# Selective scan: the column directions read runs of 8 neighbours, and copies, last spread and fifth piece stand elsewhere in the step

## The chip, the cores and the metric

The kernel runs on 1 core of a Trainium2 chip. The metric is the device time of one execution in microseconds. The core's engines are named as in the profile: PE (TensorE; PEld is its weight load), DVE (VectorE), ACT (ScalarE), POOL (GpSimd) and SP, which issues the DMAs. All data is float32.

## The reference

Eight images of 64 x 64 pixels with 96 channels go through four residual layers. Layers 0 and 2 are selective scans in four directions, layer 1 is a chunked scan, and layer 3 is a spectral layer. The change lies in layers 0 and 2:

```python
# u: [192, 64*64] after in_proj, 3x3 depthwise convolution and silu
x_wh = swapaxes(u)                       # directions 1 and 3 go down the columns
xs = stack(u, x_wh, flip(u), flip(x_wh))
dts, B, C = split(xs_k @ x_proj_k)       # 6, 16 and 16 rows for each direction k
delta = softplus(dts @ dt_w_k + bias)
h = exp(delta * A) * h + (delta * x) * B # one state for each of 192 channels x 16
y_k = sum_n h * C + D * x
y = y_0 + flip(y_2) + back(y_1) + back(flip(y_3))
x = x + out_proj(layernorm(y) * silu(z))
```

## The kernel before

**Tiles and loops.** An image's `u` and `y` stay in SBUF as `[96, 2, 4096]`: two halves of 96 channels, pixels in row order. `selective_scan` runs 32 *steps*: direction `k` from 0 to 3, and 8 chunks of 512 positions in each (`LC = 512`). For `k` 1 and 3 (the *column steps*; `wh` is true) a chunk is 8 columns of 64 pixels. `view` hands out such a chunk in the order of the scan, that is with 64 pixels of one column, 256 bytes apart, before the next column.

A step has six *units* (`n` in the loop at the end), each of 32 channels x 4 of the states on the 128 partitions and 4 groups of the states along the free axis. A unit has two scans on DVE (`scan`, L870, parts `p` 0 and 1, two groups each). The input `da` is made by ACT (`decays`, L855, two activations for each part) in PSUM, in one buffer for each part, so that the next unit's `da` can only be written when this unit's scan has read it. The other input `db` is du x B (`with_b`, L840): for units 2 and 5 POOL makes it from a copy that DMA has spread over the partitions (`du2`), for units 0, 1, 3 and 4 DVE makes it one unit ahead from `pu`, which PE spreads with two matmuls (`spread`, L834). After its scan ACT copies the last state (`leave`, L886), and POOL multiplies h by C in place (L891). `enter` (L826) puts the carried state into a later `db`.

`total_y(i, hf)` sums three units: two matmuls add the old `y` (or the skip of `u`) into `py` (L898), then 24 matmuls in eight rounds, three at a time in 32 partitions each, add h x C (L908). An ACT copy writes `py` back to `y`: L993 for the first half, L1007 for the second. The sum of units 0 to 2 is issued in unit 3, that of units 3 to 5 in unit 0 of the next step. There are 5 buffers for `h`, so unit 2 of a step takes the one that the last y sum reads.

**The next step's inputs.** `prepare(i)` is a generator that the loop calls on in parts (`prepare_part`): project `u` to the delta of the second half (four matmuls, L742) and copy it to `raw` (L747), project to the first half's delta, B and C (L751) and copy (L755), send B and C to DRAM (`bcd`, L757) and read `b` back over all partitions (four DMAs, L764), softplus (L775, with two table loads) and `dd` to DRAM, read `dx` back for three units and `c` (L782, L764), `du` on POOL (L793 in column steps, L799 in row steps) with its trip through DRAM, and the second `dx`.

**Pieces beside.** From the second image on, the spectral layer of the image before is cut into pieces (`Beside`): `begin` issues a piece's matmuls into a PSUM tile, `end` its ACT operation. A call of `selective_scan` has 139 pieces in layer 0 and 137 in layer 2, so 4 or 5 (`quota`) in each of its 32 steps.

**Order.** PSUM is full: one buffer `misc` (for `pu` and some pieces), one buffer `py` (for the y sums, the projections and the other pieces), and the two `da`. The order on each engine's queue is the order of the code below, written out by hand, and each engine works its queue in that order. In a step `i`, unit by unit, before the change:

- unit 0: spread of unit 1; last y sum of step `i - 1`; scan; L755 and `b` of step `i + 1`; scan; softplus
- unit 1: spread of unit 3; scan; L1007; a piece begins on `py`; scan; it ends; first `dx` and `c`
- unit 2: a piece begins; scan; it ends, a third begins; scan; it ends
- unit 3: spread of unit 4; first y sum; scan; scan; `du` ahead of POOL's L891
- unit 4: L993; a fourth piece begins on `misc`; L742 of step `i + 2`; scan; da of unit 5; the piece ends; scan
- unit 5: a fifth piece begins on `misc`; the last spread (unit 0 of step `i + 1`); the piece ends; scan; L747 and L751; scan; second `dx` of step `i + 1`

Of the kernel before, what the change touches and what calls it, by code (L numbers as in the profile page):

```python
# [17 lines left out]
DM = 96  # L18
# [4 lines left out]
LC = 512  # L23
# [44 lines left out]
def tile_vision_stack(  # L68
# [352 lines left out]
    def view(t, wh, at, n):  # L421
# [3 lines left out]
        return t.rearrange("p (h w) -> p w h", w=64)[:, at // 64 : (at + n) // 64, :]  # L425

    def cut(t, wh):

        return t.rearrange("p (w h) -> p w h", h=64) if wh else t
# [260 lines left out]
    def selective_scan(w, wdt, a, d, u, y, beside):  # L690
# [23 lines left out]
        with (  # L714
# [14 lines left out]
            def prepare(i):  # L729

                k, c = steps[i]
                wh, at = k % 2 == 1, c * LC
                uv = [view(u[:, hf, :], wh, at, LC) for hf in range(2)]
                m = made[i] = {"dx": [], "du": []}
# [11 lines left out]
                raw = tp.tile([128, 2, LC], F32, name="raw")  # L746
                nc.scalar.copy(raw[:DM, 1, :], pv[:DM])  # L747

# [5 lines left out]
                yield  # L754
                nc.scalar.copy(raw[:, 0, :], pv)  # L755
                bcd = dp.tile([32, LC], F32, name="bcd")
# [136 lines left out]
            def total_y(i, hf):  # L893
# [6 lines left out]
                    skip[:, hf, :] if k == 0 else ident[:DM, :DM],  # L900
                    view((u if k == 0 else y)[:, hf, :], wh, c * LC, LC),
                    start=True,
# [3 lines left out]
                for g in range(NSG):  # L906
                    for q in range(3):
                        nc.tensor.matmul(  # L908
                            py[32 * q : 32 * q + 32, :],
                            red,  # L910
                            hs[q][:, g, :],
                            start=False,
                            stop=(g == NSG - 1),
                        )
                return view(y[:, hf, :], wh, c * LC, LC), cut(py, wh)

# [16 lines left out]
            with tc.tile_pool(name="p_conv", bufs=2, space=PSUM) as pvp:  # L933
# [11 lines left out]
                for hf in range(2):  # L945
                    conv(w, y, u, (0, 8), hf)
                for _ in range(5):
                    prepare_part(0)
# [4 lines left out]
                conv(w, y, u, (8, 24), 1)  # L953
                for _ in range(2):
                    prepare_part(1)
# [7 lines left out]
            with tc.tile_pool(name="p_da", bufs=1, space=PSUM) as pap:  # L963
# [12 lines left out]
                for t in range(total + 2):  # L976
# [3 lines left out]
                    if n == 2 and quota > 1:  # L980
                        other.begin(pyp, "py")
                    elif n == 5 and quota > 4:
                        other.begin(pmp, "misc")
                    if n in (0, 3, 5) and ahead:
                        spread(t + 1)
                    elif n == 1 and t + 2 < total:
                        spread(t + 2)
                    if n == 0 and i > 0:
                        sums = total_y(i - 1, 1)
                    elif n == 3:  # L990
                        sums = total_y(i, 0)
                    elif n == 4:
                        nc.scalar.copy(*sums)  # L993
                        if quota > 3:
                            other.begin(pmp, "misc")
                        prepare_part(i + 2)
                    if n == 5:
                        other.end()
                    if t < total:
# [10 lines left out]
                    elif n == 2:  # L1010
                        other.end()
                        if quota > 2:
                            other.begin(pyp, "py")
                    elif n == 4:
                        other.end()
                    elif n == 0:
                        prepare_part(i + 1)
                    elif n == 5:
                        prepare_part(i + 2)
                    if t < total:  # L1020
# [8 lines left out]
                    if n in (1, 2):  # L1029
                        other.end()  # L1030
                    if n in (0, 1, 5):
                        prepare_part(i + 1)
# [739 lines left out]
```

## Time and profile before

| | us |
|---|---|
| time, median of 3 runs | 27056.74 (27053.37 to 27074.89) |
| the profiled execution's own time | 27082.74 |
| its span in the profile | 27080.9 |
| busy: DVE, PE, POOL, ACT | 23966.2, 22624.0, 21781.7, 16539.7 |
| L870, the scans on DVE (6144) | 13765.8 busy, 900.6 idle before |
| L891, h x C on POOL (3072) | 12769.4 busy, 726.0 idle before |
| L908, the y sums on PE (24576) | 5301.4 busy, 69.9 idle before |
| L840, db on POOL (1024) and on DVE (2048) | 4648.2 and 4643.9 busy |
| mean granted clock of PE | 0.773 of full |

The profile is of one execution; busy times are the union of an engine's instructions. "Idle before" is the engine's idle time ahead of such instructions, put down to what came last. A matmul in float32 stands as two matmul instructions.

### The profile page before, as it was taken

To read this page: it belongs to the slowest core of one execution; us is meant where nothing else is said; L and a number is where in the kernel's file an instruction comes from. 1 tells how busy PE (TensorE), PEld (TensorE's weight loads), DVE (VectorE), ACT (ScalarE), POOL (GpSimd) and SP (SyncE) were. 2 spreads that over 40 slices of the span, in tenths; PEclk is the share of its full clock that TensorE was granted. 3 is DMA by queue.
4 is the path that set the end of the run, shared out by engine and by line. 5 is a ranking of instruction groups with operands and counts; after the bars stand their busy time and mean duration, and the time that the engine had idled before them with its cause. 6 is when DMAs were issued, how large, how long until landed. Compare 5 with 4: busy or idle time off the path is not lost. (4 is left out here: it accounts for less than half of the span.)

```text
span 27080.9 us, 283056 instructions
## 1 busy us (share of the span) xinstructions
PE 22624.0 (84%) x91061; PEld 8150.5 (30%) x91061; DVE 23966.2 (88%) x17105; ACT 16539.7 (61%) x29953; POOL 21781.7 (80%) x8360
## 2 busy tenths in 40 slices
PE   7787788888888888888888888888888888888888
PEld 2141122422224222242222422224222342223424
DVE  8989899798997989979898898988989889898896
ACT  5656566466665656556565565655656556565564
POOL 8949898498984979859797697976979769797694
PEclk7687777877778777787777877778777787778878
DMA  4415454154541545415453254532545325453252
GB/s 121 119 30 124 114 130 117 31 131 122 132 111 35 133 117 137 103 44 132 116 136 98 50 132 118 135 92 56 133 119 134 85 62 133 118 134 78 70 133 67
DMA packets 1681704, 2831.72 MB, mean 105 GB/s; under 512 B 434984, under 2 KB 478280, under 8 KB 1675616
## 3 DMA queue, kind: packets, MB, share of 16 engines
q1 hardware_dynamic: 1663584, 2807.32, 41.9%
q8 instruction: 730, 11.96, 0.2%
q10 hardware_dynamic: 16640, 6.29, 0.1%
q14 instruction: 750, 6.14, 0.1%
HBM read 2385.11 MB, written 427.49 MB: 104 GB/s over the span
## 5 line engine op out<-in xcount | busy, mean ns | idle before, releaser
L870 DVE TENSOR_TENSOR_SCAN h<-da,db 128x1026 f32<-128x1026 f32 x6144 | 13765.8, 2282 | 900.6 <-ACT da L855 479.2
L891 POOL TENSOR_TENSOR h<-h,c 128x2048 f32<-128x2048 f32 x3072 | 12769.4, 4174 | 726.0 <-ACT state L886 510.1
L908 PE MATMUL py<-h,cst 128*32 128x512 f32 x24576 | 5301.4, 795 | 69.9 <-POOL h L891 69.8
L855 ACT ACTIVATE da<-dx,a2s 128x512 f32<-128x512 f32 x6144 | 4236.4, 690 | 1508.7 <-DVE h L870 1366.6
L855 ACT ACTIVATE da<-dx,a0s 128x512 f32<-128x512 f32 x6144 | 4235.8, 690 | 1481.8 <-DVE h L870 1344.3
L840 POOL TENSOR_TENSOR db<-du,b 128x2048 f32<-128x2048 f32 x1024 | 4648.2, 4539 | 567.6 <-ACT db L826 567.6
L840 DVE TENSOR_TENSOR db<-pu,b 128x2048 f32<-128x2048 f32 x2048 | 4643.9, 2268 | 110.9 <-PE pu L834 100.6
L834 PE MATMUL pu<-du,cst 32*128 32x512 f32 x4096 | 3239.2, 881 | 1007.4 <-DVE db L840 799.9
L908 PEld LDWEIGHTS py<-h,cst 128*32 128x32 f32 x24576 | 1175.0, 142 | 4827.3 <-issue 4517.4
L751 PE MATMUL pv<-u,wk 96*128 96x512 f32 x2048 | 1816.9, 1030 | 688.4 <-ACT raw L747 685.8
L898 PE MATMUL py<-y,cst 96*96 96x512 f32 x1536 | 1517.0, 1084 | 397.9 <-ACT raw L755 395.4
L834 PEld LDWEIGHTS pu<-du,cst 32*128 32x128 f32 x4096 | 790.4, 239 | 3079.7 <-issue 1361.9
L742 PE MATMUL pv<-u,wk 96*96 96x512 f32 x2048 | 1452.4, 838 | 186.7 <-ACT y L993 142.6
L1285 ACT ACTIVATE sg<-sg 128x768 f32<-128x768 f32 x1024 | 819.6, 800 | 859.1 <-PE sg L1269 859.1
L993 ACT COPY y<-py 96x512 f32<-96x512 f32 x512 | 417.5, 815 | 1411.4 <-PE py L908 1411.4
L516 PE MATMUL ps<-s,w3as 96*128 96x512 f32 x1344 | 912.4, 767 | 327.7 <-ACT sf L523 188.1
L1239 POOL TENSOR_TENSOR ce<-ec,cr 112x512 f32<-112x512 f32 x256 | 530.8, 2074 | 719.1 <-ACT ec L1237 700.8
L1317 DVE TENSOR_TENSOR wt<-wt,cbm 128x768 f32<-128x768 f32 x1024 | 985.3, 997 | 136.6 <-ACT wt L1286 136.1
L886 ACT COPY state<-h 128x4 f32<-128x4 f32 x3072 | 597.5, 194 | 782.5 <-DVE h L870 776.8
L751 PEld LDWEIGHTS pv<-u,wk 96*128 96x128 f32 x2048 | 540.6, 291 | 1740.2 <-ACT raw L747 1212.5
L319 POOL TENSOR_SCALAR xn<-xs,sb 96x512 f32<-96x512 f32 x192 | 198.1, 1033 | 991.7 <-PE pz L324 495.6
L1216 POOL TENSOR_TENSOR rr<-lr,cc 128x768 f32<-128x768 f32 x256 | 376.6, 1471 | 754.1 <-ACT lr L1214 749.2
(241 smaller groups left out, 30790.9 us busy)
## 6 DMA issues: line engine op xcount, KB each, us to landing
dx<-dd SPq DMA_DIRECT2D x4096, 192.0 KB
b<-bcd SPq DMA_DIRECT2D x2048, 256.0 KB
c<-bcd SPq DMA_DIRECT2D x2048, 256.0 KB
du<-dud SPq DMA_DIRECT2D x2048, 128.0 KB
dd<-raw SPq DMA_DIRECT2D x1024, 192.0 KB
dud<-du SPq DMA_DIRECT2D x512, 128.0 KB
xd<-xs SPq DMA_DIRECT2D x256, 192.0 KB
cr<-bcd SPq DMA_DIRECT2D x1536, 32.0 KB
```

What stands on the lines that cost most here:

```text
L516: nc.tensor.matmul(ps, w3as[:, m * 128 : (m + 1) * 128], live["x2"], start=True, stop=True)
L742: nc.tensor.matmul(pv[:DM], weights[k][:, hi, 128:], uv[hi], start=(hi == 0), stop=(hi == 1))
L751: nc.tensor.matmul(pv, weights[k][:, hi, :128], uv[hi], start=(hi == 0), stop=(hi == 1))
L834: nc.tensor.matmul(pu, sel[rows, :], m["du"][rows, n // 3, :], start=True, stop=True)
L840: (nc.gpsimd if pool else nc.vector).tensor_mul(groups(m["db", n]), (m["du2"][:, n // 3, :] if pool else m["pu"]) .unsqueeze(1) .to_broadc ...
L855: nc.scalar.activation(dst[:, g, :LC], made[i]["dx"][n // 3][:, n % 3, :], AF.Exp, scale=av4[:, k, n, gs : gs + 1],)
L870: nc.vector.tensor_tensor_scan(made[i]["h", n][:, at][:, way], das[p][:, rev : 2 * SEG + rev][:, way], made[i]["db", n][:, at][:, way], 0. ...
L891: nc.gpsimd.tensor_mul(h, h, made[i]["c"])
L898: nc.tensor.matmul(py, skip[:, hf, :] if k == 0 else ident[:DM, :DM], view((u if k == 0 else y)[:, hf, :], wh, c * LC, LC), start=True, st ...
L908: nc.tensor.matmul(py[32 * q : 32 * q + 32, :], red, hs[q][:, g, :], start=False, stop=(g == NSG - 1),)
L1285: nc.scalar.activation(sg, sg, AF.Abs)
L1317: nc.vector.tensor_mul(it["wt"], it["wt"], m["cbm"][:, j : j + 1, :].to_broadcast([128, RK, Q]),)
```

## The change

In column steps, `near` reads and writes `u` and `y` row by row with runs of 8 neighbours, so `pv` and `py` hold a chunk in the order of the pixels' rows. The order of the scan is restored elsewhere: L747 and L755 read `pv` in PSUM at every eighth element (`turn_back`), and L908 writes `py` in PSUM at every eighth element, 64 elements for each of 8 columns. The copies of `py` to `y` then read PSUM in order and write runs of 8. Row steps keep their access.

In all steps, L993 stands behind the da of unit 5; L742, L747, L751 and L755 have four parts of their own, in units 4 and 5 of the step two ahead, so that L755, `bcd` and `b` come at the end of unit 5, ahead of the second `dx`; the last spread stands in unit 4, behind the beginning of the fourth piece; and the fifth piece runs on `py` from the end of unit 2 to the middle of unit 3.

```diff
+    def near(t, wh, at, n):
+        if not wh:
+            return t[:, at : at + n]
+        return t.rearrange("p (h w) -> p h w", w=64)[:, :, at // 64 : (at + n) // 64]
+
+    def turn_back(t, wh, n):
+        return t.rearrange("p (h w) -> p w h", w=n // 64) if wh else t
...
-                uv = [view(u[:, hf, :], wh, at, LC) for hf in range(2)]
+                uv = [near(u[:, hf, :], wh, at, LC) for hf in range(2)]
...
-                nc.scalar.copy(raw[:DM, 1, :], pv[:DM])
+                nc.scalar.copy(cut(raw[:DM, 1, :], wh), turn_back(pv[:DM], wh, LC))
+                yield
...
-                nc.scalar.copy(raw[:, 0, :], pv)
+                nc.scalar.copy(cut(raw[:, 0, :], wh), turn_back(pv, wh, LC))
...
-                    view((u if k == 0 else y)[:, hf, :], wh, c * LC, LC),
+                    near((u if k == 0 else y)[:, hf, :], wh, c * LC, LC),
...
-                            py[32 * q : 32 * q + 32, :],
+                            turn_back(py[32 * q : 32 * q + 32, :], wh, LC),
                             red,
-                            hs[q][:, g, :],
+                            cut(hs[q][:, g, :], wh),
...
-                return view(y[:, hf, :], wh, c * LC, LC), cut(py, wh)
+                py = py.rearrange("p (h w) -> p h w", h=64) if wh else py
+                return near(y[:, hf, :], wh, c * LC, LC), py
...
-                for _ in range(5):
+                for _ in range(6):
                     prepare_part(0)
...
-                for _ in range(2):
+                for _ in range(4):
                     prepare_part(1)
...
                     if n == 2 and quota > 1:
                         other.begin(pyp, "py")
-                    elif n == 5 and quota > 4:
-                        other.begin(pmp, "misc")
-                    if n in (0, 3, 5) and ahead:
+                    if n in (0, 3) and ahead:
                         spread(t + 1)
...
                     elif n == 4:
-                        nc.scalar.copy(*sums)
                         if quota > 3:
                             other.begin(pmp, "misc")
+                        if t + 2 < total:
+                            spread(t + 2)
                         prepare_part(i + 2)
-                    if n == 5:
-                        other.end()
+                    elif n == 5:
+                        prepare_part(i + 2)
                     if t < total:
                         scan(t, 0)
...
+                    elif n == 3:
+                        other.end()
                     elif n == 4:
+                        nc.scalar.copy(*sums)
                         other.end()
-                    elif n == 0:
-                        prepare_part(i + 1)
-                    elif n == 5:
-                        prepare_part(i + 2)
...
                     if n in (1, 2):
                         other.end()
+                        if n == 2 and quota > 4:
+                            other.begin(pyp, "py")
+                    if n in (4, 5):
+                        prepare_part(i + 2)
                     if n in (0, 1, 5):
                         prepare_part(i + 1)
```

## The prediction

> **What bounds the kernel now.** I read the page's busy rows first, then busy time in single stretches, then the waits, then the timeline of one step.
>
> ```profile
> span 27080.9 us, 283056 instructions
> PE 22624.0 (84%) x91061; PEld 8150.5 (30%) x91061; DVE 23966.2 (88%) x17105; ACT 16539.7 (61%) x29953; POOL 21781.7 (80%) x8360
> ```
>
> Two engines stand near the top, but this mixes stages. The sixteen selective scans (first to last L870 of each call) add up to 19,215 us, 37.53 us for each of 512 steps. Eight column steps and eight row steps of one call:
>
> ```profile
> core 0: us, PE busy (x) PEld busy (x) DVE busy (x) ACT busy (x) POOL busy (x), PEclk, DMA share, GB/s
> 7110.00:7410.00 300.00, 263.91 (x785) 79.82 (x785) 286.04 (x130) 208.93 (x387) 293.06 (x73) 0.75 0.54 132
> 7410.00:7710.00 300.00, 255.89 (x785) 81.09 (x784) 285.23 (x129) 204.44 (x387) 291.76 (x73) 0.74 0.53 132
> ```
>
> POOL is busy 97%, DVE 95%; over all calls POOL has 18,493 us (36.12 per step). So nothing below about 36.1 to 36.7 us per step can come from waits: nine POOL instructions a step (six L891 of 4.14 each in a chain, two L840 of 4.54, du of 2.40 or, in columns, 2.88) are 36.3 in rows and 36.8 in columns. What can be won is DVE's remaining idle:
>
> ```profile
> DVE h L870 <- ACT da L855: 479.2, 563, 7.8
> DVE h L870 <- PE py L908: 184.8, 276, 1.1
> ACT y L993 <- PE py L908: 1411.4, 477, 6.6
> ACT y L1007 <- PE py L908: 258.7, 261, 10.9
> ```
>
> Sorting the timeline's idle ahead of L870 and L840 by unit: unit 5's first scan waits 258.5 us for da, unit 2's first scan 184.8 for py (its h buffer is read by the last y sum) and 72.6 for da, unit 0's db (L840, issued in unit 5) 85.9 for pu. Unit 4 (94.5) and unit 3 (47.4) are few long waits. The timeline shows the first of these in a column step:
>
> ```profile
> 7211.30 4.48 DVE L870 TENSOR_TENSOR_SCAN h<-da,db 128x1026 f32<-128x1026 f32 x2
> 7214.99 1.07 ACT L993 COPY y<-py 96x512 f32<-96x512 f32 x1 [4.33 <-PE py L908]
> 7215.85 1.41 ACT L855 ACTIVATE da<-dx,a0s 128x512 f32<-128x512 f32 x2
> 7216.67 3.59 PE L742 MATMUL pv<-u,wk 96*96 96x512 f32 x4
> 7217.35 4.48 DVE L870 TENSOR_TENSOR_SCAN h<-da,db 128x1026 f32<-128x1026 f32 x2 [1.57 <-ACT da L855]
> ```
>
> ACT stands at the y copy while da for unit 5, whose input was free at 7213.6, queues behind it; DVE then idles 1.57 us. A row step, for the sizes:
>
> ```profile
> 339.33 0.58 ACT L993 COPY y<-py 96x512 f32<-96x512 f32 x1 [3.86 <-PE py L908]
> ...
> 339.97 1.96 PE L742 MATMUL pv<-u,wk 96*96 96x512 f32 x4 [0.75 <-ACT y L993]
> ```
>
> The same four L742 take 1.96 us in rows and 3.59 in columns, the copy 0.58 and 1.07. Over the run L742 has 592 ns (median) in rows, 1035 in columns; at half clock both read about 1060.
>
> **Part by part.**
>
> *Copies, last spread.* The y copy moves behind unit 5's first da, L755 from unit 0 to the end of unit 5, the last spread from unit 5 to unit 4. Unit 5's wait (258.5) goes: the copy no longer stands before da. The last y sum starts when POOL's sixth L891 ends and not when L755 does: at 350.77 against 352.39 + 1.96 in the row step, 3.6 us earlier, more than unit 2 waited (at most 1.1 each). So 184.8 goes, and 72.6 with it, since L1007 then finds py done. The last spread is issued some 5 us ahead of its need, so 85.9 goes. Together 601.8 us.
>
> *What these moves put in the way.* In unit 4 PE's queue now holds the fourth piece, the spread (its buffer is free when ACT has read that piece, after da and the y copy), then four L742 (free after the y copy), and ACT waits for them in L747 ahead of the next step's first da. From the column step above without its stall: da to 7215.1, copy 0.58 and piece about 0.5 to 7216.1, spread 1.12 (full clock) or 2.07 (half), L742 1.96 or 3.65, L747 0.57, da 1.42: 7221.2 or 7223.8. DVE wants it at 7211.3 + 4.4 + 4.4 + 2.4 = 7222.5. So 1.3 us early or 1.3 late. Behind the waiting L747 on ACT stand both da of the next unit 0 and the state copy that POOL's L891 waits for; the clock of 0.74 to 0.75 means half of the time at half clock. I take 0.5 us for the 7 x 64 = 448 steps with pieces: 224 us; between 0 and 1.3 x 448 = 582. The first image's 64 steps have no piece and no cost. L747 also overwrites raw, which POOL's du reads until 7214.3, five us before: no cost. The two parts more ahead of each call's loop stand beside the convolution and cost nothing.
>
> *Fifth piece.* 139 and 137 pieces on 32 steps give 11 and 9 steps with five, 140 in all. It stood ahead of the last spread and made the 85.9 us; now it stands on py ahead of unit 4's spread and the first y sum. Who waits is unit 4's db. I price it at what it cost before, 86 us (bounds 0 and 140 x 2 us).
>
> *SP's queue.* The four b copies (1.73 us of issue, 1 MB) now go before the four dx copies, behind bcd. Packets moved 230 to 250 KB per us after b's issue, so b holds the queue 4.3 us. dx is wanted two units and one scan (some 14 us) later, and bcd's trip (1.7), b (4.3 + 1.2) and dx (3.2 + 1.2) need 11.6. Nothing on the path, with 2 us to spare; if that cover goes, 1 us per step.
>
> *Columns.* Twelve matmuls (L742, L751, L898) read runs of 8 instead of one element every 256 bytes: between 0 and 12 x 0.44 = 5.3 us of PE per column step at full clock. Two y copies save up to 0.47 each. L747 and L755 read PSUM at every eighth element: 0.58 to 1.05 each. All this is beside the path, where ACT (70%) and PE (88%) have room; it shortens the late chain above, and I count it at nothing.
> The Trainium skill, "SBUF — State Buffer", Door 1, says that SBUF works in lines of 16 bytes and that two hits per line suffice; runs of 8 floats have four, so by it the whole 5.3 us comes.
>
> *The price of it:* 48 L908 per column step now write PSUM at every eighth element. No row shows a matmul that does so. Bounds: nothing; or what strided reading showed, never faster than half clock, eight rounds of 0.86 = 6.9 us per sum instead of 4.8 to 6.0. The first sum's room is from 7210.1 to the copy's new place at 7215.6, the last one's from POOL's L891 to unit 2's first scan, 8 us. I take no cost on the path, because half of these matmuls run at half clock already and reads lose nothing there; the other end is the first rival.
> "PSUM — Partial Sum Buffer", Specifications, states lines of 8 bytes and that any non-contiguous pattern slows matmuls significantly. That speaks against this change; by it the sum is the first rival's.
>
> *Sum.* 601.8 - 224 - 86 = 292 us. With 0.57 us off a step DVE meets POOL, which leaves 0.8 in column steps at most; I take a quarter off: 220 us. The profiled execution (27,082.7, span 27,080.9) would be near 26,863; against the median of 27,056.7 that is 26,840.
>
> **Rivals.**
>
> *Strided writing slows the sums (slower).* In the column step the first sum ends at 7217.0 or later, the y copy holds ACT past it, unit 5's second da comes 1.4 us late, L742 starts later and at half clock, and the next da is 1.5 to 2.6 late: about 3 us per column step with pieces and 1 without, 224 x 3 + 32 = 700 us. Rows keep half the gain: 27,057 - 110 + 700 = 27,650. It decides once a round takes over 0.7 us on average in the first sum; at 1.7 us a round both sums are 7 us late or more and 29,500 is near. For it: the strided reads. Against: PE loses 5.3 us of work beside it.
>
> *New waits take all.* The L747 chain late in every step (582) and the fifth piece (86) exceed 602: 27,120. For it: PE works on nothing for 2 us before the spread, and the clock is 0.74; against: L742 in rows ran at full clock before.
>
> *Runs of 8 read no faster.* Then columns gain nothing on PE; the moves remain: about 26,900.
>
> **How the numbers follow.** A measurement can tell 0.2%, 54 us, from no change: under 27,003 or over 27,111. Forecast 60% (26,560 to 27,000: the bounds are all 602 won, less POOL's limit, and 60 left), third rival 3%, new waits 13% (27,000 to 27,150: 2 faster, 6 same, 5 slower), strided writing 24% (27,111 to 29,500). Faster 65%, same 6%, slower 29%. The range 26,560 to 27,700 leaves out 4% below and some 11% above.
>
> **What would show it.** Right: L870's wait for da under 300 us and for py under 50; L742 near 592 ns in columns at full clock; L993 at 0.6 us in columns; L993 waiting under 400 us; steps of the first image at 36.5. Wrong: L908 in columns at 850 ns and more at full clock, PE busy above 84%, L747 waiting for L742 in most steps, or unit 3's db waiting for pu over 150 us.

## The result, and the profile after

The changed kernel takes 27,509.3 us (median of 4 runs, 27,502.0 to 27,532.1) against 27,065.8 us for the kernel before in the same comparison (27,053.4 to 27,079.7). The ratio is 1.0165, 95% interval 1.0148 to 1.0183: 1.65% slower, where 0.8% faster was forecast. The time lies inside the stated range, with the opposite sign.

The page's first lines, and the two groups in which DVE's and POOL's idle time can be read (line, engine, operation, tiles; busy us, mean ns; idle us before it and its main releaser). The line numbers have moved by 10 to 35: L870 is now L881, L891 is L902, L840 is L851, L834 is L845, L742 is L752, L747 is L757, L755 is L766, L993 is L1028 and L1007 is L1018.

```profile
span 27530.3 us, 283336 instructions
PE 22137.1 (80%) x91061; PEld 8558.9 (31%) x91061; DVE 23986.9 (87%) x17105; ACT 16339.9 (59%) x29953; POOL 21788.5 (79%) x8360
...
L881 DVE TENSOR_TENSOR_SCAN h<-da,db 128x1026 f32<-128x1026 f32 x6144 | 13762.4, 2282 | 918.9 <-ACT da L866 507.8
L902 POOL TENSOR_TENSOR h<-h,c 128x2048 f32<-128x2048 f32 x3072 | 12761.2, 4171 | 1115.3 <-issue 631.1
L851 DVE TENSOR_TENSOR db<-pu,b 128x2048 f32<-128x2048 f32 x2048 | 4646.8, 2269 | 523.1 <-PE pu L845 513.6
```

PE has 487 us less to do. DVE's and POOL's work is what it was, so the span can only have grown by idle time between their instructions. POOL's idle before h x C went from 726.0 to 1115.3 us, and db on DVE, which hardly waited, now waits 513.6 us for pu. The sixteen scan calls add up to 19,656.6 us, 38.39 us a step against 37.53: 442 us more, of the 449 us between the two profiled executions (27,532.1 and 27,082.7).

The waits (waiter, released by: us in total, times, longest), for the pairs that the prediction read before:

```profile
DVE h L881 <- ACT da L866: 507.8, 510, 7.8
DVE h L881 <- PE py L919: 87.0, 149, 1.1
ACT y L1028 <- PE py L919: 191.1, 268, 1.8
ACT y L1018 <- PE py L919: 195.7, 63, 12.7
ACT raw L757 <- PE pv L752: 930.2, 473, 6.6
```

The y copy's wait has gone from 1411.4 to 191.1 us and the scans' wait for py from 184.8 to 87.0, as meant. In their place ACT stands 930 us at L757 waiting for L752, and the scans' wait for da has not become smaller.

**The same idle time by unit.** The timeline's idle ahead of the scans and of db, sorted by the unit in which it falls:

| DVE waits | before, us | after, us | after, first image | after, steps of five pieces |
|---|---|---|---|---|
| unit 5, first scan, for da | 258.5 | under 1 | under 1 | under 1 |
| unit 2, first scan, for py, da, and unnamed | 257.4 | 180.7 | 22.0 | 47.4 |
| unit 5, db of unit 0, for pu | 85.9 | under 1 | under 1 | under 1 |
| unit 3, db of unit 4, for pu | 14.6 | 513.6 | 0 | 418.7 |
| unit 5, second scan, for da | 5.7 | 227.5 | 0 | 105.7 |
| unit 3, second scan, for da | 47.4 | 90.0 | 0 | 61.7 |
| unit 5, first scan, for py | under 2 | 47.5 | 0 | 35.7 |
| unit 0, first scan, for da | under 2 | 50.4 | 1.9 | 17.2 |

Added up over all units, DVE's waits ahead of the scans and of db in the scan calls went from 787 to 1,234 us: 447 us more, about as much as the calls grew (442). Of the 601.8 us of waits that were to go some 420 went. Unit 5's two waits are gone, but unit 2's first scan still waits 180.7 of 257.4 us, 109.2 of them for nothing that the profile names. Hardly anything new comes in the first image, which has no pieces: its steps fell from 37.3 to 36.2 us. These are eight row steps and eight column steps of it (window, length, busy us of each engine, granted clock, DMA share, GB/s):

```profile
core 0: us, PE busy (x) PEld busy (x) DVE busy (x) ACT busy (x) POOL busy (x), PEclk, DMA share, GB/s
124.50:414.90 290.40, 188.15 (x519) 47.45 (x519) 283.99 (x129) 189.05 (x353) 282.51 (x72) 0.73 0.52 126
414.90:706.20 291.30, 200.28 (x545) 50.44 (x545) 284.04 (x128) 188.32 (x352) 291.30 (x72) 0.74 0.55 132
```

By these windows a step takes 36.3 us in rows and 36.4 in columns, with POOL 97% and 100% busy. With pieces it is the other way round: steps with four pieces went from 37.2 to 37.7 us on average (308 steps, some 143 us in all), steps with five from 38.2 to 40.9 (140 steps, 370 us). So the loss lies in the steps with pieces, and most of it in those that have a fifth.

This is a step with a fifth piece in the kernel after, units 2 and 3 (start us, length, engine, line; idle before and releaser in brackets):

```profile
7022.00 0.63 SPq L461 DMA_DIRECT2D sx<-xd  x1
...
7029.02 0.81 ACT L466 ACTIVATE sn<-sx,sb 96x512 f32<-96x512 f32 x1 [7.71 <-DMA sx<-xd]
7029.74 1.39 ACT L866 ACTIVATE da<-dx,a0s 128x512 f32<-128x512 f32 x2
...
7029.89 0.85 PE L474 MATMUL ps<-cst,sn 96*64 96x96 f32 x4 [9.10 <-ACT sn L466]
...
7030.66 2.07 PE L845 MATMUL pu<-du,cst 32*128 32x512 f32 x2
...
7032.77 2.29 DVE L851 TENSOR_TENSOR db<-pu,b 128x2048 f32<-128x2048 f32 x1 [8.01 <-PE pu L845]
```

The fifth piece's input (`sx`) was asked for at 7022.00, at the end of unit 2 in the order of the code, and comes 7 us later. Its matmuls (L474) hold PE's queue until then, and the spread of unit 4 (L845) stands behind them, though nothing that it needs is late; db waits 8.01 us. ACT stands just as long at L466, which prepares that input, with unit 4's da (L866) behind it. So PE's queue is not the only one that the piece holds.

And the second new wait, in unit 4 of another step:

```profile
7263.99 0.58 ACT L1028 COPY y<-py 96x512 f32<-96x512 f32 x1 [1.51 <-PE py L919]
...
7264.97 0.69 ACT L533 ACTIVATE sf<-ps,w3bs 128x512 f32<-128x512 f32 x1 [0.40 <-PE ps L526]
...
7265.73 1.42 ACT L866 ACTIVATE da<-dx,a0s 128x512 f32<-128x512 f32 x2
...
7267.18 2.29 DVE L881 TENSOR_TENSOR_SCAN h<-da,db 128x1026 f32<-128x1026 f32 x1 [0.89 <-ACT da L866]
```

The y copy has passed unit 5's first da and now stands, with the fourth piece's operation behind it, ahead of the second. It still waits for the y sum, and the scan that waits is the second instead of the first.

### The profile page after: what moved, and what is told of

Same layout as the page of the kernel before. It is cut to its first block, busy times and chain, and to the rows that moved or that the text cites. A ratio compares the mean times of both kernels' runs of the same rounds, so it can differ in the third digit from the quotient of the medians.

```text
span 27530.3 us, 283336 instructions
## 1 busy us (share of the span) xinstructions
PE 22137.1 (80%) x91061; PEld 8558.9 (31%) x91061; DVE 23986.9 (87%) x17105; ACT 16339.9 (59%) x29953; POOL 21788.5 (79%) x8360
## 5 line engine op out<-in xcount | busy, mean ns | idle before, releaser
L881 DVE TENSOR_TENSOR_SCAN h<-da,db 128x1026 f32<-128x1026 f32 x6144 | 13762.4, 2282 | 918.9 <-ACT da L866 507.8
L902 POOL TENSOR_TENSOR h<-h,c 128x2048 f32<-128x2048 f32 x3072 | 12761.2, 4171 | 1115.3 <-issue 631.1
L919 PE MATMUL py<-h,cst 128*32 128x512 f32 x24576 | 5225.5, 738 | 396.4 <-POOL h L902 396.0
L866 ACT ACTIVATE da<-dx,a0s 128x512 f32<-128x512 f32 x6144 | 4239.4, 690 | 1581.2 <-DVE h L881 1409.6
L866 ACT ACTIVATE da<-dx,a2s 128x512 f32<-128x512 f32 x6144 | 4240.2, 690 | 1528.6 <-DVE h L881 1378.9
L851 DVE TENSOR_TENSOR db<-pu,b 128x2048 f32<-128x2048 f32 x2048 | 4646.8, 2269 | 523.1 <-PE pu L845 513.6
L851 POOL TENSOR_TENSOR db<-du,b 128x2048 f32<-128x2048 f32 x1024 | 4649.5, 4541 | 565.8 <-ACT db L837 565.8
L845 PE MATMUL pu<-du,cst 32*128 32x512 f32 x4096 | 2952.2, 807 | 1469.8 <-DVE db L851 915.4
L919 PEld LDWEIGHTS py<-h,cst 128*32 128x32 f32 x24576 | 1168.8, 132 | 4832.5 <-issue 3855.9
L845 PEld LDWEIGHTS pu<-du,cst 32*128 32x128 f32 x4096 | 738.3, 224 | 3120.1 <-DVE db L851 1594.2
L526 PE MATMUL ps<-s,w3as 96*128 96x512 f32 x1344 | 1129.7, 935 | 650.9 <-ACT y L1018 324.9
L762 PE MATMUL pv<-u,wk 96*128 96x512 f32 x2048 | 1276.9, 755 | 394.9 <-ACT raw L757 394.9
L909 PE MATMUL py<-y,cst 96*96 96x512 f32 x1536 | 1269.2, 921 | 10.2 <-ACT y L1028 4.5
L752 PE MATMUL pv<-u,wk 96*96 96x512 f32 x2048 | 1168.3, 699 | 57.6 <-DMA wk<-wdt 18.9
L546 PE MATMUL ps<-w3bs,sf 128*128 128x96 f32 x5376 | 1140.5, 373 | 0.0
L546 PEld LDWEIGHTS ps<-w3bs,sf 128*128 128x128 f32 x5376 | 1062.0, 286 | 0.0
```

What stands on the lines that cost most here:

```text
L526: nc.tensor.matmul(ps, w3as[:, m * 128 : (m + 1) * 128], live["x2"], start=True, stop=True)
L546: nc.tensor.matmul(po, live["f"][m][:, at : at + 128], w2q[:, m, :], start=False, stop=(m == 2),)
L752: nc.tensor.matmul(pv[:DM], weights[k][:, hi, 128:], uv[hi], start=(hi == 0), stop=(hi == 1))
L762: nc.tensor.matmul(pv, weights[k][:, hi, :128], uv[hi], start=(hi == 0), stop=(hi == 1))
L845: nc.tensor.matmul(pu, sel[rows, :], m["du"][rows, n // 3, :], start=True, stop=True)
L851: (nc.gpsimd if pool else nc.vector).tensor_mul(groups(m["db", n]), (m["du2"][:, n // 3, :] if pool else m["pu"]) .unsqueeze(1) .to_broadc ...
```

## The experiments

Two theories were tested. A: the order of the work around the pieces costs the time, the fifth piece above all. B: PE's writing and ACT's reading of PSUM at every eighth element cost it. The line numbers in a run are its own. Each set of runs had the kernel before beside it, with medians of 27,098.6 us (first four runs), 27,099.5, 27,082.2 and 27,097.4 us (last four); ratios are to these.

### Taking the change apart

**e1: the fifth piece alone, on the order before**

```diff
                     if n == 2 and quota > 1:
                         other.begin(pyp, "py")
-                    elif n == 5 and quota > 4:
-                        other.begin(pmp, "misc")
...
-                    if n == 5:
-                        other.end()
...
-                    elif n == 4:
+                    elif n in (3, 4):
                         other.end()
...
                     if n in (1, 2):
                         other.end()
+                        if n == 2 and quota > 4:
+                            other.begin(pyp, "py")
```

> The kernel before with one part of the change alone: the fifth piece begins on py at the end of unit 2 and ends in the middle of unit 3; columns, copies, projections and the last spread stay as before. Theory A (the loss comes from the fifth piece, whose matmuls wait for the piece before it and for their DMA ahead of the spread of unit 4 on PE): DVE's db waits for pu by over 300 us in all, up from about 100 in the kernel before, nearly all of it in steps of five pieces, and the time is about 27,350 us (27,250 to 27,450). Theory B (the loss comes from PE writing and ACT reading PSUM at every eighth element in column steps): nothing of that is in here, so about 27,065 us, or about 86 us less, since the wait of unit 0's db behind the piece in unit 5 goes.

Measured: 27,483.3 us, ratio 1.0139 (1.0124 to 1.0155), 385 us more, with no change to a column. The time is above A's range, and db's wait for pu falls short of the 300 us that A asked for. All the same the loss is there, and all of it in steps of five pieces (38.2 to 41.0 us; those of four stay at 37.2). So A stands in kind, and B can't be the cause of this part. DVE's waits:

```profile
DVE h L870 <- ACT da L855: 669.1, 588, 7.2
DVE db L840 <- PE pu L834: 274.0, 91, 6.6
```

Of the 274 us, 268.9 are in unit 3; the 85.9 us in unit 5 are 5.1 now. The scans' wait for da grew by 190 us: unit 5's first scan waits 484.5 instead of 258.5, because the first y sum, which needs py, starts behind the fifth piece, and the y copy and da follow it.

**e3: the columns alone**

The six edits of the change that use `near` and `turn_back`, and nothing else.

> The kernel before with the column accesses alone changed (runs of 8 in the projections, in y's addition and in the copies; PSUM written and read at every eighth element); the order of the work stays. Theory A: the column accesses cost nothing; with the shorter y copy ahead of the scans, 27,000 us (26,920 to 27,070). Theory B: most of the loss is here, 27,300 to 27,500 us.

Measured: 26,853.3 us, ratio 0.9909 (0.9892 to 0.9925), 245 us less, below A's range. B falls. The strided accesses cost nothing and the shorter projections and copies are worth more than expected; this kernel beats both. The gain is in steps with pieces alone: those of the first image take 37.3 us as before. Two of its groups:

```profile
L1004 ACT COPY y<-py 96x512 f32<-96x512 f32 x512 | 297.8, 582 | 1361.5 <-PE py L918 1361.5
L752 PE MATMUL pv<-u,wk 96*96 96x512 f32 x2048 | 1013.9, 618 | 135.9 <-ACT y L1004 93.0
```

The first y copy had a mean of 815 ns, L742 of 838 ns. By the sorting of idle time the wait of unit 0's db behind the fifth piece in unit 5 fell from 85.9 to 7.2 us (PE reaches that piece sooner, since L742 ahead of it is shorter) and unit 5's wait for da from 258.5 to 177.1: 160 of the 161 us by which DVE's waits fell.

**e2: the fifth piece and the last spread back in unit 5, the rest of the change kept**

```diff
-                    if n in (0, 3) and ahead:
+                    elif n == 5 and quota > 4:
+                        other.begin(pmp, "misc")
+                    if n in (0, 3, 5) and ahead:
                         spread(t + 1)
...
-                        if t + 2 < total:
-                            spread(t + 2)
                         prepare_part(i + 2)
                     elif n == 5:
                         prepare_part(i + 2)
+                        other.end()
...
-                    elif n == 3:
-                        other.end()
...
-                        if n == 2 and quota > 4:
-                            other.begin(pyp, "py")
```

> The kernel after with the fifth piece and the last spread put back into unit 5 as in the kernel before; all else of the change stays. Theory A: the 514 us in which DVE's db waits for pu fall below 150, and the time falls by about 350 us to 27,150 us (27,050 to 27,250). Theory B: the columns are untouched, so about 27,500 us. A third reading, that the last spread and not the fifth piece makes the wait, gives the same time here and is told apart by the run of the fifth piece alone.

Measured: 27,007.6 us, ratio 0.9968 (0.9955 to 0.9981), 502 us below the kernel after as the medians stand, 1.97% by the ratios, and better than A's range. db still waits 188.1 us for pu in all, where under 150 was expected. Against the columns alone, the moves of the copies and projections are left in it, and they cost 0.59%, some 160 us. They cost it in steps with pieces; those of the first image take 36.2 us, as in the kernel after.

**e5: the last spread alone back in unit 5**

```diff
-                    if n in (0, 3) and ahead:
+                    if n in (0, 3, 5) and ahead:
                         spread(t + 1)
...
-                        if t + 2 < total:
-                            spread(t + 2)
```

> The kernel after with the last spread alone put back into unit 5; the fifth piece stays on py between units 2 and 3. The two together were worth 502 us (27,509 against 27,008), and the fifth piece alone cost 385 us on the order of the kernel before. If the fifth piece is nearly all of it here too: 27,390 us (27,300 to 27,480), with DVE's db still waiting for pu in unit 3 for over 300 us. If the last spread in unit 4 is the larger part: about 27,010 to 27,150 us.

Measured: 27,344.7 us, ratio 1.0090 (1.0075 to 1.0105), the first reading; db still waits 439.9 us in unit 3. The spread's own 0.75% can be seen on POOL: its h x C of unit 5 was idle 219 us in the kernel after, 193 of them with the scan done and the state copy not, and is idle 18 us here. In unit 4 the spread stood on PE ahead of L752 and waited until ACT had read the fourth piece; L757 waited on ACT for L752 (930.2 us in the kernel after, 139.3 here), and the next da and the state copy behind L757.

So the change comes apart, by ratios, step by step from the kernel before:

| step | ratio | part |
|---|---|---|
| columns (e3) | 0.9909 | -0.91% |
| + copies and projections moved (e2) | 0.9968 | +0.59% |
| + fifth piece moved (e5) | 1.0090 | +1.22% |
| + last spread moved (the kernel after) | 1.0165 | +0.75% |

Each ratio has some 0.15% of uncertainty on either side, so each part some 0.2%. On the order before, the fifth piece alone was worth 1.39%.

### What the fifth piece costs

**e8: the fifth piece behind the spread of unit 4**

```diff
                     elif n == 3:
+                        if quota > 4:
+                            other.begin(pyp, "py")
                         sums = total_y(i, 0)
...
-                        if n == 2 and quota > 4:
-                            other.begin(pyp, "py")
```

> The kernel after with one pair exchanged on PE's queue: in steps of five pieces the fifth piece begins behind the spread of unit 4 instead of ahead of it, still on py and still ahead of the first y sum. If its matmuls, waiting ahead of the spread, are what makes db late: db's wait for pu in unit 3 falls from 514 us below 150, and the time to about 27,250 us (27,150 to 27,350), as the sum now starts late in its place. If pieces in quick succession are the matter wherever they stand: the wait turns up as da of unit 4 or the y sum in unit 5, and the time stays above 27,400 us.

Measured: 27,500.7 us, ratio 1.0148 (1.0132 to 1.0163): no gain. db's wait in unit 3 fell to 132.4 us as expected, and the second reading holds all the same: the y sum is late now, and unit 5's first scan waits 323.3 us for py (47.5 before this exchange).

```profile
DVE h L881 <- ACT da L866: 596.5, 583, 7.4
...
DVE h L881 <- PE py L919: 355.4, 208, 3.8
DVE db L851 <- PE pu L845: 132.4, 93, 2.0
```

The place on PE's queue only decides who waits. What is late is the piece.

**e13 and e15: the pieces' loads issued earlier.** `Beside.ahead` walks the list of pieces and stops at the first one that has no load until that one is next. So a load that may be issued four pieces ahead is issued one or two ahead, where pieces without a load come first.

```diff
-                if self.loaded > k + (op[5] if op and op[0] else 0):
+                if self.loaded > k + (op[5] if op and op[0] else 4):
```

e13 is e1 with this line, e15 the kernel after with it.

> The kernel before with the fifth piece moved, and the loads of the pieces issued up to four pieces ahead also where pieces without a load lie between (until now such a load is issued when the last of these has become the next piece). The fifth piece alone cost 385 us, and three of its eighteen kinds of steps, which cost 6.5 to 7.9 us each, begin it while sx or sc is still on its way. If the transfers are the whole of it: the 269 us of db's wait for pu fall below 80 us and the time to 27,150 us or less. If they are only those three kinds of steps (3 x 7 x 7 = 154 us) and the rest is the fifth tenant on the one buffer py, ahead of the first y sum: about 27,330 us (27,250 to 27,400). If they are nothing: 27,460 us or above.

> The kernel after with the same earlier loads. If the fifth piece's transfers cost about what they cost on the order of the kernel before (154 us): about 27,350 us (27,270 to 27,430), with db's wait for pu in unit 3 down from 514 to about 300 us. If they are all of that wait: 27,100 us. If they are nothing: 27,500 us.

Measured: e13 27,332.6 us, ratio 1.0088 (1.0073 to 1.0104), and e15 27,331.3 us, 1.0086 (1.0071 to 1.0101), both times at the middle reading: by the ratios the earlier loads are worth 0.51% in e1 and 0.79% in the kernel after, 151 and 178 us as the medians stand. In e15 db's wait in unit 3 fell only to 418.2 us, where some 300 were expected. Unit 4's first scan waits 46.5 us there instead of 94.5, as it does in e14 below (43.5), so not all of the 178 us need be the fifth piece's. The same step (the 18th of layer 0 of the third image), first in e1, then in e13:

```profile
7537.36 1.79 SPq L764 DMA_DIRECT2D c<-bcd  x4
...
7539.25 0.45 SPq L495 DMA_DIRECT2D sc<-x1d  x1
...
7546.31 1.99 PE L499 MATMUL ps<-updown,sc 64*96 64x128 f32 x8 [6.28 <-DMA sc<-x1d]
7548.23 2.07 PE L834 MATMUL pu<-du,cst 32*128 32x512 f32 x2
...
7550.34 2.29 DVE L840 TENSOR_TENSOR db<-pu,b 128x2048 f32<-128x2048 f32 x1 [5.64 <-PE pu L834]
```

```profile
7496.51 1.33 PE L499 MATMUL ps<-updown,sc 64*96 64x128 f32 x8 [1.05 <-ACT sg L564]
7497.77 2.07 PE L834 MATMUL pu<-du,cst 32*128 32x512 f32 x2
...
7500.03 2.27 DVE L840 TENSOR_TENSOR db<-pu,b 128x2048 f32<-128x2048 f32 x1
```

In e1 sc is asked for behind the four copies of c and is there 7 us later; PE waits 6.28 us and db 5.64. In e13 PE only waits for the piece before. The step takes 38.5 us instead of 44.7. Of the eighteen kinds of steps with five pieces (a kind is the same step of the same layer in seven images; the last step of a call is left out) just three fell, from 45.4, 44.6 and 44.9 us to 38.6, 38.5 and 38.3 (medians); the others are as in e1, up to some 4 us above the kernel before. That rest, 235 us in e13, is not a transfer: no operation waits for sx or sc any more (164.4 and 89.3 us in e1), and the waits for the pieces' other inputs, sr and s, are 165.9 and 71.7 us, where the kernel before has 168.8 and 97.9. It fits the fifth piece being one more tenant of py ahead of the first y sum: unit 5's first scan still waits 492.8 us for da behind the y copy (258.5 before), and unit 3's db 147.6 us for pu (14.6 before). No run gave the piece another buffer at this place.

**e14: the columns alone with the same earlier loads**

> The kernel before with the column accesses alone and the same earlier loads. Here the fifth piece stands in unit 5 and its transfers have landed, so both readings expect little: 26,853 us, or up to 60 us less where unit 3 and unit 4 wait for a piece's transfer (142 us in 42 long waits), or some 40 us more if the earlier loads hold the queue of SP ahead of dx and c.

Measured: 26,838.7 us, ratio 0.9907 (0.9892 to 0.9921), not to be told from e3. With the fifth piece in its old place, two units later, its transfers were covered.

### What the moved copies cost

**e6: the columns, and the y copy in the middle of unit 4**

```diff
                     elif n == 4:
-                        nc.scalar.copy(*sums)
                         if quota > 3:
...
                     elif n == 4:
+                        nc.scalar.copy(*sums)
                         other.end()
```

> The kernel before with the column accesses and one move: the copy of the first y sum stands in the middle of unit 4, behind the first da of unit 5. With the column accesses alone, unit 5's first scan waits 177 us for da. If that wait goes and less than half comes back at the second scan of unit 5: about 26,760 us (26,700 to 26,830). If the second da of unit 5 behind the copy and the fourth piece's operation takes all of it back, as the 167 us of that wait in the run with the fifth piece and the last spread put back would say: 26,850 us or above, to 26,950.

Measured: 27,026.2 us, ratio 0.9973 (0.9961 to 0.9984), 0.64% above e3: the second reading or worse, for another reason than the one given. Unit 5's first scan no longer waits for da (177.1 us before), and its second waits only 66.2. But db of unit 0 waits 229.8 us for pu, which was 7.2:

```profile
PE pv L752 <- ACT y L1025: 744.0, 384, 5.0
...
DVE db L850 <- PE pu L844: 240.7, 221, 4.2
```

L752 needs py free, so it now waits 744.0 us for the later copy (93.0 in e3), and the last spread is behind it on PE.

**e16: the same, with L742 behind the last spread**

```diff
-                        prepare_part(i + 2)
                     if n == 5:
+                        prepare_part(i + 2)
                         other.end()
```

> The kernel before with the column accesses, the copy of the first y sum in the middle of unit 4, and L742 behind the last spread in unit 5 instead of ahead of it in unit 4. With the copy alone moved (27,026 us against 26,853), unit 0's db waited 230 us for pu, whose spread stood on PE behind L742, which waits for that copy. If this is why the copy's move cost time: that wait falls below 60 us and the time to about 26,800 us (26,720 to 26,870). If the time goes on ACT, where L747 now waits for L742: 26,950 us or above.

Measured: 27,246.3 us, ratio 1.0052 (1.0035 to 1.0069), 220 us worse than e6. The wait in unit 5 fell to 42.3 us, as expected for PE's queue; and ACT pays, as the second reading has it:

```profile
ACT raw L757 <- PE pv L752: 841.7, 316, 6.7
...
DVE db L850 <- PE pu L844: 442.2, 346, 2.0
```

L757 waits for L752 in 316 steps, the second projection goes to PE late, and the db that waits is the one made in unit 0 (389.1 us of the 442.2).

**e7: the columns, and L755 at the end of unit 5**

```diff
-                    elif n == 0:
-                        prepare_part(i + 1)
...
+                    if n == 5:
+                        prepare_part(i + 2)
                     if n in (0, 1, 5):
                         prepare_part(i + 1)
```

(with one part more ahead of the loop)

> The kernel before with the column accesses and one move: the second copy of the projections (L755) with bcd and b stands at the end of unit 5, ahead of the second dx, and the first copy and the second projection stay in the middle of unit 5. With the column accesses alone, unit 2's first scan waits 174 us for the last y sum, whose matmuls begin behind that copy. If the earlier copy frees the sum: below 40 us of that wait and about 26,720 us (26,650 to 26,800). If the time goes to da of unit 0 or 1 behind the copy on ACT: 26,850 us or above.

Measured: 27,192.7 us, ratio 1.0037 (1.0024 to 1.0050), 1.3% above e3. The wait of unit 2's first scan for the last y sum is gone (174.3 us in e3), and far more has come:

```profile
ACT y L1004 <- PE py L918: 1946.9, 478, 6.8
...
DVE h L880 <- ACT da L865: 787.1, 750, 8.1
ACT raw L765 <- PE pv L761: 788.0, 512, 3.9
```

At the end of unit 5 the second projection was begun only a scan earlier, so the copy L765 stops ACT in all 512 steps, 1.54 us each, with the next da and the state copies behind it. Unit 5's first scan waits 495.2 us for da.

**e4: the kernel e2, with the fourth piece's operation behind the second da of unit 5**

```diff
                         nc.scalar.copy(*sums)
-                        other.end()
...
-                    if n in (1, 2):
+                    if n in (1, 2, 4):
                         other.end()
```

> The kernel after with the fifth piece and the last spread back in unit 5, and the ACT operation that ends the fourth piece moved from the middle of unit 4 to its end, behind both da of unit 5. Theory A with its second half (the second da of unit 5 is late, 228 us in the kernel after, since the y copy and the fourth piece's operation stand ahead of it on ACT): 130 to 200 us below the run with the fifth piece and the last spread put back, so about 26,980 us (26,850 to 27,100). If the y copy alone makes that da late, no different from that run. Theory B: about 27,500 us.

Measured: 26,986.4 us, ratio 0.9956 (0.9941 to 0.9971), not separable from e2 (0.9968). That this is near the 26,980 expected is luck: e2 came out lower than thought, and the 130 to 200 us below it did not come. The 167.2 us of the second scan's wait are gone, and db's wait for pu in unit 5 rose from 110.7 to 253.2 us, which fits the piece holding `misc` longer, since the fifth piece and the last spread need that buffer.

### Is PE's chain the limit, or ACT's queue?

POOL's idle time in the scan calls of e3 (516 us) is mostly waiting for a state copy of a scan that has ended: 195 us in unit 1 and 120 in unit 2, where the copy stands on ACT behind operations that wait for PE. Three runs on e3 and one on the kernel after moved the state copy ahead of them. The edit for unit 2, and the like for unit 1:

```diff
-                    elif n == 2:
-                        other.end()
-                        if quota > 2:
-                            other.begin(pyp, "py")
...
                         scan(t, 1)
                         leave(t, n == 3)
+                    if n == 2:
+                        other.end()
+                        if quota > 2:
+                            other.begin(pyp, "py")
```

> The kernel before with the column accesses, and on ACT's queue the copies of the last state in units 1 and 2 stand ahead of the copy of the second y sum (unit 1) and ahead of the end of the second piece (unit 2), with the beginnings of the pieces that follow them moved along. With the column accesses alone, POOL is idle 516 us in the scan calls, 316 of them waiting in units 1 and 2 for the state copy though the scan has ended. If ACT's queue, held by operations that wait for PE, is what bounds the step through POOL: that part falls below 120 us and the time to about 26,650 us (26,560 to 26,750). If PE is the limit in units 0 to 2 (y sum and three pieces), the later pieces give it back: 26,800 us or above.

> The kernel before with the column accesses, and in unit 2 alone the state copy stands ahead of the end of the second piece and the beginning of the third. Theory of ACT's queue: of the 120 us in which POOL waits for this copy in unit 2 about 100 go: 26,750 us (26,690 to 26,830). Theory of PE as the limit: no gain, 26,850 us or above.

> The kernel before with the column accesses, and in unit 1 alone the state copy stands ahead of the copy of the second y sum and the beginning of the first piece. Theory of ACT's queue: of the 195 us in which POOL waits for this copy in unit 1 about 150 go: 26,700 us (26,640 to 26,790). Theory of PE as the limit: the first piece begins up to 1 us later, the chain of three pieces ends later in unit 2, and POOL waits there instead: 26,850 us or above.

> The kernel after with one exchange on ACT's queue: in unit 2 the state copy stands ahead of the end of the second piece and the beginning of the third. In the kernel after POOL waits 527 us in unit 2 for the state copy though the scan has ended. Theory of ACT's queue: that falls below 150 us; with half of it given back by the fifth piece beginning later, about 27,320 us (27,150 to 27,420). Theory of PE as the limit, or of the fifth piece as the whole: the wait of db for pu in unit 3 grows by as much, and the time stays at 27,500 us or above.

Measured: e9 27,080.2 us, ratio 0.9999 (0.9990 to 1.0008); e10 27,072.4, 0.9996 (0.9986 to 1.0006); e11 26,862.3, 0.9918 (0.9903 to 0.9932); e12 27,619.3, 1.0196 (1.0181 to 1.0212). The theory of ACT's queue lost four times. In e10 POOL's idle ahead of h x C fell from 141 to 13 us in unit 2, as it said, and rose from 274 to 504 in unit 1:

```profile
POOL h L901 <- ACT state L896: 655.5, 581, 3.7
DVE h L880 <- ACT da L865: 501.7, 498, 6.8
...
DVE h L880 <- PE py L918: 252.6, 338, 1.4
```

(367.0, 405.0 and 174.3 us in e3.) In e3 the second piece's operation begins 0.2 us before unit 2's second scan ends (mean of the steps with pieces). In e10 it stands behind the state copy, which waits for that scan; so the third piece begins 0.8 us later and the first y sum 0.45 us later. The 219 us that this costs are 0.49 us for each of the 448 steps with pieces, about as much as the y sum is late. In e12 the unit 3 wait of db rose from 513.6 to 580.8 us. In e11 the second y copy and the first piece come later; POOL's unit 1 gained 157 us and its unit 2 lost 199, and the time stayed. So ACT's order can't be mended by itself; that PE is the limit is not shown by these runs, since the later pieces wait for ACT too.

## Why the prediction was wrong

**The step that failed** is the price of the fifth piece: "I price it at what it cost before, 86 us (bounds 0 and 140 x 2 us)". It measured 385 us on the order before and 1.22% (330 us) as the step from e2 to e5, above the upper bound. In the sum the move even stood at nothing, 85.9 us won in unit 5 against 86 paid, and the 385 us are what it cost with that gain in it. Both halves of the price were wrong. The old 86 us were not the piece's own, for with shorter projections ahead of it they fell to 7.2 (e3). And the new place took away two covers that the text did not name: the two units in which its transfer landed, worth 151 us in e1 (e13) and up to 178 in the kernel after (e15), and the freedom of py, which the first y sum needs next (the rest, some 235 us, argued from e8 and e13 and not isolated).

**A second step failed with it**: the sum took the removed waits, 601.8 us, as gains that add up. Some 420 us of them went, and in the first image, without pieces, the whole change was worth 1.1 us a step (36.2 us, where 36.5 was forecast). With pieces the copies and projections are links of one chain: y sum, y copy, L742, L747, L751, L755, next y sum and three pieces all take turns in the single buffer py. Moving the y copy alone cost 0.64% (e6) and moving L755 alone 1.3% (e7), although each removed the wait it was aimed at; both moves together, with the projections in their new parts, cost 0.59% (e2), less than the two alone would add up to. So the costs do not add up any more than the gains. What these moves put in the way was looked for in one place, L747. That the shared buffer py makes the chain is read from the waits of e6, e7, e10 and e16; no run had a second one.

**L747's chain** was right in kind and size. 224 us were set against it; ACT waits 930 us at L757, in 473 steps, and the last spread's move, which makes that chain (139 us of that wait without it, e5), costs 0.75%, 203 us. But the sum gave that spread 85.9 us of gain, and e3 shows that these could be had without it.

**The second da of unit 5** (227.5 us after, 5.7 before) had no term in the sum; only the first rival names it, for a late sum. The sign was to be read in the text's own column step: the copy and the piece were followed as far as the spread, L742 and L747, and not to the da that stands between them on the same queue.

**The columns** were counted at nothing on the path and gave 245 us. The work taken away lies within the bounds and below their upper end: in e3 the durations of L742, L751 and L898 in columns add up to 2,715 us against 3,297, which is 2.3 us a column step and not 5.3. L751 and L898 gave little of it (medians of 1061 ns in e3, in rows and in columns; 1042 and 1062 in columns before). That it is beside the path was wrong, since L742 and the y copy are links of the same chain; which of the two gave how much was not separated.

**The strided PSUM accesses** cost nothing, as taken. L919 has a median of 593 ns in columns and in rows, with means of 735 and 740 (L908 in columns had 617 and a mean of 793); L757 takes 581 ns reading every eighth element of PSUM and 581 in order. The first rival, with the right sign and 24%, has the wrong mechanism: e3 refutes it. "PSUM — Partial Sum Buffer", Specifications, in the Trainium skill has non-contiguous patterns slow matmuls significantly; these matmuls, in float32 with runs of one element, do not show it. The rule in "SBUF — State Buffer", Door 1, agrees for one of the three groups of matmuls: L752 with runs of 8 has a median of 592 ns in columns, where L742 with single elements had 1035.

**The rival of new waits** (13%) was the right one in kind, and stopped at 27,120 because it took the fifth piece at 86 us and had no term for the second da; its 582 us for L747's chain were too much (203).

**The signs.** Right as listed: L752 at 592 ns, the y copy at 0.58 us in columns and waiting 191.1 us, first image at 36.2. Of the signs of being wrong, two came: L757 waits for L752 in most steps, and unit 3's db waits over 150 us. The scans' waits, expected below 300 us for da and 50 for py, are 507.8 and 87.0.

**The better kernel** is the smallest part of the change: columns alone, 26,853 us (0.9909), with every operation in its old place.

## What to carry to other kernels

Where several kinds of work take turns in one PSUM buffer, a wait in the trace is a place where a chain is seen, not a cost that can be subtracted: before moving a copy, list who has the buffer next and what stands behind each of them on every queue, and try first to shorten its links: in this kernel shorter links paid and moved ones cost. A filler piece has two prices that do not move with it: how long ago its input was asked for, and whose buffer it holds. A stretch without fillers (here the first image) shows what an order is worth by itself; if it gains there and loses elsewhere, the fillers are the matter.

## What the runs showed of the hardware

A small transfer, sc, issued behind c's four copies and dx's four, reached PE 7 us later (7539.25 to 7546.31 in e1). Asked for earlier (e13) it held nobody up: the step took 38.5 us instead of 44.7. PE writing PSUM at every eighth float32 ran at a median of 593 ns a matmul, as it did in order (L919), while reading single float32 elements 256 bytes apart in SBUF took 1035 ns against 592 in order (L742).
